# The last two groups' (p x) Wv^T and two more groups' M x in Strassen form, and x1's rows transposed by VectorE and DRAM instead of TensorE

## The chip, the cores and the metric

The kernel runs on one core of a Trainium2 chip. The metric is the device time of the whole program in microseconds, as a median over runs. All data are 32-bit floats. TensorE (PE) does matrix products into PSUM banks of 128 x 512 numbers; VectorE (DVE), ScalarE (ACT) and GpSimd (POOL) do the rest[...]. DMAs are issued from three in-order queues, on SyncE (SP), ACT and POOL, and share 16 DMA engines.

## The reference, cut to what matters

N = 4096 nodes, D = 512 features, H = 128 hidden. Layer 0 is attention with the adjacency matrix added to its scores (twice, as spatial and as edge encoding), then a residual and a layer norm. Layer 1 is a two-layer graph convolution, again with residual and layer norm.

```python
q = x @ Wq.T + bq;  k = x @ Wk.T + bk;  v = x @ Wv.T + bv
a = q @ k.T / sqrt(D) + adj + adj
x1 = layernorm(x + softmax(a) @ v)
h = relu(adj @ (x1 @ W1) + b1)
out = layernorm(x1 + adj @ (h @ W2) + b2)
```

## The kernel before, in words

Queries are taken in 8 groups of 512 (`g`), keys in 8 blocks of 512 (`d`) or 16 pairs of 256 (`q`). Scores are x M x^T with M = Wk^T Wq, so that group g needs `u = M x` (with a bias `ub_t`), 512 x 512. Almost every product is a Strassen-Winograd product: seven half-size products (`ORDER` 1, 2, 6, 7, 5, 4, 3) in place of eight; 1, 6, 5 and 3 go into one PSUM bank (X), 2 and then 7 and 4 into another (Y), and the bank is read out between products. A right-hand operand has seven parts (`B11` ... `T4`), a left-hand one seven others.

*Startup.* Wq and Wk are transposed on TensorE (L848), M is formed (L856, `psm`), and then u of group 0 by plain products (`u_products`, L262, 16 products of 128 x 512). Groups 2 to 7 get their u from `u_fast` (L234, 28 products of 128 x 256, from sums of M in `m_sums`), group 1 from `u_products`, all as filler between the score products of group 0. The parts of u go to DRAM (`store_u`, L176 and L178) and are loaded when their group comes. `sum_x` (L349) forms sums of x for later, in three slots of `t_sb`.

*Groups.* The program is a list of units, each with seven places; a group lasts 16 units. At each place TensorE does one half of a score product (`qk`, L436; VectorE reads it at L449). `hooks` put other work at a given unit and place. `work` is a list of filler items, each with an estimated time, dealt out evenly over the places: the products p x of the previous group (`px_items`, L576, 224 items of 0.43 us, over 128 x 256) and, first among them, the rows of the group before that one's end (`row_items`, L754). Softmax (shift L479, exponential L483, sums L492) and the sums for p x (L519 to L531) are hooks.

*Rows.* For groups 0 to 5 (`FAST_V`) `rows_out_fast` (L659) does (p x) Wv^T in Strassen form: `s3` and three other sums on VectorE, 28 products of 128 x 256 (L703), read by VectorE at L671. Groups 6 and 7 use `rows_out` (L642): 16 products of 128 x 512 (L651). A group has four row tiles (`r`) of 128 rows. Each is normed (`rows_norm`, ACT), gets b2 and goes to DRAM (`add_b2`), is transposed by four TensorE transposes into a bank (`project`, L740) and copied out by ACT (L742, tile `x1t`), and multiplied by W1 into `t_sb` (`project2`, L749). Group 7's rows run inside layer 1: `put(n, ...)` places them beside product n of its first block, with the single bank `m1`.

*Layer 1* is a row of Strassen blocks (L1041) with loads of adj^T and sums on VectorE (L1008 to L1016), then plain products (L1342), the product with W2 and the last norm.

## Time and profile before

| | |
|---|---|
| median of 3 runs | 2306.16 us (2304.3 to 2306.61) |
| the profiled execution, and its span | 2308.84 us, 2307.1 us |
| TensorE products busy | 2276.3 us, 99% of the span |
| VectorE, GpSimd, ScalarE busy | 1617.0, 1018.7, 399.8 us |
| moved by DMA | 525.14 MB, 228 GB/s over the span |
| TensorE clock granted | 0.998 |

A product of two 32-bit operands is two matrix records in the profile, a transpose is one. Records overlap, so the cost of one is the distance between starts, not its own duration. A line such as `PE x1ps L740 <- ACT xr L639: 2.3, 6, 0.4` in the view of waits says: TensorE, at line 740, waited for line 639 on ACT for 2.3 us in total, 6 times, 0.4 us at most. In windows, (x94) is the number of instructions.

### The profile page before, as it was taken

What the parts mean: (1) busy time and instruction counts of PE and PEld (TensorE: products, weight loads), DVE (VectorE), ACT (ScalarE), POOL (GpSimd) and SP (SyncE); (2) the same over time, 40 slices, a digit from 0 to 9 for tenths busy, and PEclk for the clock granted to TensorE, in tenths of its full rate; (3) what the DMA queues carried; (4) which work ended last, traced back from release to release, by engine and by line L of the source; (5) the groups of instructions that cost most, each with busy time, mean ns of one, the idle gap of its engine ahead of it and who ended that gap; (6) DMA issues with size and microseconds to landing.
All of it is one profiled execution on the core that took longest, in us unless ns stands there. A gap on an engine that the chain in (4) does not pass through costs nothing.

```text
span 2307.1 us, 28475 instructions
## 1 busy us (share of the span) xinstructions
PE 2276.3 (99%) x10672; PEld 1750.6 (76%) x10672; DVE 1617.0 (70%) x2276; ACT 399.8 (17%) x438; POOL 1018.7 (44%) x1009
## 2 busy tenths in 40 slices
PE   9999999999999999999999999999999999999998
PEld 5888788888888888888888888888876743333456
DVE  4676776687667756765776687568657877888864
ACT  2212211131122112111311121122102000000012
POOL 3565654185327424731653274237429830001043
PEclk9999999999999999999999999999999999999999
DMA  6999878667857684777578586947754468899996
GB/s 177 273 284 309 233 215 230 193 174 215 246 135 218 189 246 114 215 213 215 151 221 232 145 218 193 259 117 210 196 191 155 155 237 321 332 347 375 352 383 218
DMA packets 282711, 525.14 MB, mean 228 GB/s; under 512 B 23184, under 2 KB 130448, under 8 KB 281680
## 3 DMA queue, kind: packets, MB, share of 16 engines
q1 hardware_dynamic: 229040, 406.12, 52.3%
q0 software_dynamic: 43296, 105.39, 20.7%
q10 hardware_dynamic: 10240, 11.82, 1.7%
q8 instruction: 85, 1.39, 0.2%
q14 instruction: 50, 0.41, 0.0%
HBM read 475.27 MB, written 46.41 MB: 226 GB/s over the span
## 4 chain that ended last, share of the span: by engine, by line
PE 92%; DVE 4%; POOL 2%; DMA 1%; issue 1%; ACT 0%; SPq 0%; POOLq 0%; DVEq 0%; ACTq 0%
PE p L576 32%; PE X L436 18%; PE b L1041 15%; PE Y L436 14%; PE v L703 3%; PE acce L1342 2%; PE psu L234 2%; PE ops L1296 1%; PE tps L749 1%; PE psu L262 1%; PE x L651 1%; PE x1ps L740 1%; DVE s L449 1%; PE psm L856 1%; DMA u_d<-uo 1%
## 5 line engine op out<-in xcount | busy, mean ns | idle before, releaser
L576 PE MATMUL p<-s,xn 128*128 128x256 f32 x3584 | 895.6, 380 | 7.0 <-DVE s L531 2.6
L576 PEld LDWEIGHTS p<-s,xn 128*128 128x128 f32 x3584 | 677.1, 190 | 111.0 <-DVE s L531 5.6
L436 PE MATMUL X<-ut,sa 128*128 128x256 f32 x1984 | 513.4, 381 | 1.7 <-DVE s L449 1.7
L492 POOL TENSOR_TENSOR lacc<-lacc,s 128x512 f32<-128x512 f32 x240 | 344.1, 1434 | 203.2 <-ACT s L483 192.3
L436 PEld LDWEIGHTS X<-ut,sa 128*128 128x128 f32 x1984 | 370.1, 190 | 64.2 <-DVE s L449 15.3
L449 DVE TENSOR_TENSOR s<-X,s 128x512 f32<-128x512 f32 x256 | 176.3, 689 | 278.6 <-PE X L436 278.2
L436 PE MATMUL Y<-ut,sa 128*128 128x256 f32 x1408 | 361.6, 380 | 0.2 <-DVE s L449 0.2
L436 PEld LDWEIGHTS Y<-ut,sa 128*128 128x128 f32 x1408 | 266.8, 190 | 37.7 <-issue 1.4
L483 ACT ACTIVATE s<-s 128x1024 f32<-128x1024 f32 x128 | 135.3, 1057 | 790.3 <-DVE s L479 790.3
L458 DVE TENSOR_TENSOR macc<-macc,s 128x512 f32<-128x512 f32 x240 | 258.1, 1075 | 1.2
L449 DVE TENSOR_TENSOR s<-Y,s 128x512 f32<-128x512 f32 x192 | 131.9, 687 | 157.0 <-PE Y L436 155.7
L479 DVE TENSOR_TENSOR s<-s,mb 128x512 f32<-128x512 f32 x256 | 231.2, 913 | 2.4 <-ACT mb L399 2.4
L385 POOL DMA_DIRECT2D s<-in_adjT_dram x64 | 84.4, 1318 | 256.7 <-ACT s L380 255.9
L549 DVE TENSOR_TENSOR ot<-p,ot 128x512 f32<-128x512 f32 x248 | 168.9, 681 | 31.4 <-PE p L576 31.2
L1008 DVE TENSOR_TENSOR tt<-ck 128x1024 f32<-128x1024 f32 x112 | 138.4, 1270 | 38.7 <-PE b L1041 33.6
L1041 PE MATMUL b<-tt,st 128*64 128x512 f32 (+1 forms) x768 | 156.0, 541 | 0.0
L380 ACT COPY s<-cb 128x2048 f32<-128x2048 f32 x64 | 121.0, 1890 | 48.1 <-PE p L576 39.8
L519 POOL TENSOR_TENSOR s<-s 128x256 f32<-128x256 f32 x128 | 124.6, 974 | 0.6
L1041 PEld LDWEIGHTS b<-tt,st 128*64 128x64 f32 x768 | 53.9, 137 | 87.8 <-issue 79.9
L526 DVE TENSOR_TENSOR s<-s 128x512 f32<-128x512 f32 x128 | 114.3, 914 | 0.0
L520 POOL TENSOR_TENSOR s<-s 128x256 f32<-128x256 f32 x128 | 107.8, 842 | 10.0
L489 POOL TENSOR_TENSOR lacc<-s 128x512 f32<-128x512 f32 x8 | 10.6, 1321 | 197.9 <-ACT s L483 197.9
(186 smaller groups left out, 2112.6 us busy)
## 6 DMA issues: line engine op xcount, KB each, us to landing
ck<-in_adjT_dram SPq DMA_DIRECT2D x128, 1024.0 KB, 7.4
s<-in_adjT_dram POOLq DMA_DIRECT2D x64, 1024.0 KB, 11.5
sa<-s_d SPq DMA_DIRECT2D x224, 256.0 KB, 5.7
xn<-in_x_dram SPq DMA_DIRECT2D x192, 256.0 KB, 4.3
xn<-xs_d SPq DMA_DIRECT2D x96, 512.0 KB, 5.7
sa<-in_xT_dram SPq DMA_DIRECT2D x168, 256.0 KB, 4.7
xn<-xs_d SPq DMA_DIRECT2D x64, 256.0 KB, 3.9
ut<-u_d SPq DMA_DIRECT2D x49, 256.0 KB, 7.2
```

The source lines that it names most:

```text
L380: nc.scalar.copy(s, CB[g].unsqueeze(1).to_broadcast([P, 4, W]))
L436: nc.tensor.matmul(T["X" if k in (1, 6, 5, 3) else "Y"][:, ts(j, HW)], SA[g, d, a][:, c, j, :], UT[g, b][:, c, :], start=k in (1, 2, 7) an ...
L449: nc.vector.tensor_tensor(ck, ps, ck, ALU.add)
L458: nc.vector.tensor_tensor(MACC[g], MACC[g], ck[:, h, :], ALU.max)
L479: nc.vector.tensor_tensor(ck, ck, MB[g], ALU.subtract)
L483: nc.scalar.activation(ck, ck, AF.Exp, scale=2.0)
L492: nc.gpsimd.tensor_tensor(LACC[g], LACC[g], ck[:, h, :], ALU.add)
L519: nc.gpsimd.tensor_tensor(b12, b12, b11, ALU.subtract)
L549: nc.vector.tensor_tensor(to, ps, to, ALU.add)
L576: nc.tensor.matmul(T["PX" if k in (1, 6, 5, 3) else "PY"][:, ts(f, HW)], XN[n][:, q - a, ts(f, P)], quarters(g, q)[{1: 0, 2: 2, 6: 1, 7: 0 ...
L1008: nc.vector.tensor_tensor(t[:, :2], v[:, :, 1], v[:, 0], ALU.subtract)
L1041: nc.tensor.matmul(BK[n][k][ts(half, HH)], lhs, right(u, i, half, b), start=q == 0, stop=q == NP - 1,)
```

## The change

It has four parts.

1. `FAST_V` covers all eight groups. Group 6 uses `rows_out_fast` in its old place; its sums go to GpSimd (`sum_`). Group 7 uses it beside layer 1's first block with `alone`: order 2, 1, 6, 5, 3, 7, 4, all in the bank `m1`, each product read (`j == 2`) two places after it is issued and the next issued two places later.
2. For groups 0 to 5 the transposes leave TensorE. `turn_blocks` lets VectorE transpose the sixteen 32 x 32 blocks of each 128-column part; `store_blocks` writes them to DRAM in four DMAs on SP whose runs are 32 numbers (128 bytes), which puts the blocks in their places; `load_blocks` loads the row tile back. This is moved 70 and more items later in the list.
3. u of groups 0 and 1 also comes from `u_fast`; group 0's directly into its operands. The sums of M, the scores' first sums and the constants of group 0 move into the startup, whose products are reordered. The tile of u is stored in other pieces: B21 by itself from ACT's queue, the rest two products earlier than before.
4. In group 0, `sum_x` is loaded two units ahead instead of one, with five slots instead of three, and `store_s` is issued later.

```diff
-    FAST_V = range(NG - 2)
+    FAST_V = range(NG)
...
+        if what == B21:
+            nc.scalar.dma_start(u_d[b][:, what], UO[b][what])
...
-            nc.gpsimd.dma_start(u_d[b][:, 1:6], UO[b]["all"])
+            nc.gpsimd.dma_start(u_d[b][:, 2:6], UO[b]["all"])
...
+                if b:
+                    store_u(b, B11)
+                    store_u(b, "all")
             if k == 3:
-                store_u(b, "all")
+                if b:
+                    store_u(b, B21)
...
+        sum_ = (nc.gpsimd if g >= NG - 2 else nc.vector).tensor_tensor
...
+        if j == 2:
+            read(k)
+            if k == 1:
+                sum_(a11, a21, a11, ALU.subtract)
+                sum_(a12, a12, a11, ALU.subtract)
+            if k in (3, 4):
+                stats(0 if k == 3 else 2)
+            return
+        if (k, j) == ((2, 0) if alone else (1, 0)):
             read_px()
             T["s3"] = rowp.tile([P, 2, HW], F32, tag="x1t", name=f"s3_{g}")
-            tt(T["s3"], a11, a21, ALU.subtract)
-            tt(a21, a21, a22, ALU.add)
+            sum_(T["s3"], a11, a21, ALU.subtract)
+            sum_(a21, a21, a22, ALU.add)
...
+    def turn_blocks(g, r):
+        T["x1t", g, r] = rowp.tile([P, ND, P], F32, tag="x1t", name=f"x1t{g}_{r}")
+        nc.vector.transpose(T["x1t", g, r].rearrange("p c i -> p (c i)"), XR[g][:, r, :])
+
+    def store_blocks(g, r):
+        x1t = T.pop(("x1t", g, r))
+        to = xt_d[g, r].rearrange("(b i) c (a j) -> a i c b j", i=32, j=32)
+        for a in range(4):
+            nc.sync.dma_start(
+                to[a], x1t[ts(a, 32)].rearrange("i c (b j) -> i c b j", j=32)
+            )
+
+    def load_blocks(g, r):
+        T["x1t", g, r] = XR[g][:, r, :].rearrange("p (c i) -> p c i", i=P)
+        nc.sync.dma_start(T["x1t", g, r], xt_d[g, r])
...
+        if g < NG - 2:
...
+                *w(1), item(0, rows_last, g), *norm(2), *norm(3), *w(8), *norm(0), *w(2), *norm(1), *w(70),
+                *b2(2), *w(3), *turn(2), *w(5), *store(2), *b2(3), *w(11), *turn(3), *load(2), *w(5),
+                *store(3), *b2(0), *w(11), *turn(0), *load(3), *pro2(2), *w(5), *store(0), *b2(1),
+                *w(11), *turn(1), *load(0), *pro2(3), *w(5), *store(1), *w(11), *load(1), *pro2(0),
+                *w(14), *pro2(1),
...
-    first = u_products(0)
...
+    for f in u_fast(0):
...
-    work[0] = 3, [(0.86, f) for f in u_products(1)]
-    work[3] = 13, [(0.86, f) for g in range(2, NG) for f in u_fast(g)] + [(0, lambda: owing.pop()())] * 2
+    work[1] = 15, [(0.86, f) for g in range(1, NG) for f in u_fast(g)] + [(0, lambda: owing.pop()())] * 2
...
-        at(2 * d, 1, store_s, d)
+        at(2 * d + 1, 0, store_s, d)
...
-        at(max(q - 1, 0), 0, sum_x, q)
+        at(max(q - 2, 0), 0, sum_x, q)
...
+    for n, k in enumerate((2, 1, 6, 5, 3, 7, 4)):
+        for j in range(2):
+            put(8 + 4 * n, rows_out_fast, g, k, j, True)
+        put(10 + 4 * n, rows_out_fast, g, k, 2, True)
     for r in range(PER):
-        for c in range(ND):
-            put(9 + 6 * r, rows_out, g, r, c)
...
-        put(35 + 6 * r, project, g, r)
-        put(38 + 6 * r, project2, g, r)
-    put(60, sum_t, 8, 14, 16)
...
+        put(46 + 5 * r, project, g, r)
+        put(49 + 5 * r, project2, g, r)
+    put(66, sum_t, 8, 14, 16)
```

## The prediction

> **What bounds the kernel now.** I read the page first (busy shares, slices, chain), then TensorE's waits, then windows by stage.
>
> ```profile
> PE 2276.3 (99%) x10672; PEld 1750.6 (76%) x10672; DVE 1617.0 (70%) x2276; ACT 399.8 (17%) x438; POOL 1018.7 (44%) x1009
> ...
> PE 92%; DVE 4%; POOL 2%; DMA 1%; issue 1%; ACT 0%; SPq 0%; POOLq 0%; DVEq 0%; ACTq 0%
> ```
>
> TensorE is busy from 3.99 us on, at a granted clock of 0.998, and is 92% of the chain: a product taken away is worth its own time wherever nothing else then ends last. Only 2307.1 - 2276.3 = 30.8 us are idle, and the waits name about half of that (in the view of waits: total, times, longest):
>
> ```profile
> PE X L436 <- DVE s L449: 4.1, 5, 1.0
> ...
> PE x1ps L740 <- ACT xr L639: 2.3, 6, 0.4
> PE psu L234 <- ACT uo L211: 1.9, 1, 1.9
> PE x1ps L740 <- ACT x1t L742: 1.5, 1, 1.5
> ...
> PE x L651 <- DVE xr L656: 0.9, 1, 0.9
> PE tps L749 <- ACT x1t L742: 0.7, 1, 0.7
> ```
>
> The timeline gives the prices (start us, us):
>
> ```profile
> 29.21 10.47 PE L262 MATMUL psu<-xt,m_t 128*128 128x512 f32 x24
> 39.52 1.03 PE L436 MATMUL X<-ut,xt 128*128 128x256 f32 x4
> 40.38 1.02 PE L262 MATMUL psu<-xt,m_t 128*128 128x512 f32 x2
> ...
> 1736.09 0.60 PE L740 MATMUL x1ps<-ident,xr 128*128 128x128 f32 x4
> 1736.53 1.03 PE L576 MATMUL p<-s,xn 128*128 128x256 f32 x4
> ```
>
> Twelve products of 512 columns (two records each) take 39.52 - 29.21 = 10.31, so 0.86 each; two of 256 (four records) 0.86, so 0.43 each; a row tile's four transposes 0.44.
>
> **The change, part by part.**
>
> *Products.* 16 of 0.86 (13.76) become 28 of 0.43 (12.04): -1.72 for each of four groups (u of 0 and 1, rows of 6 and 7), -6.9. *Transposes:* 24 tiles of groups 0 to 5, 24 x 0.44 = -10.6; `project2` stays. Together -17.4 us of TensorE work.
>
> *Waits that go.* The six of 0.4 before L740 (-2.3). The waits 1.5 and 0.7 of group 6, whose norms and transposes get twelve px items between them instead of six, and the 0.9 on the bank of `rows_out` (-3.1). The 1.9 at L234 is ACT waiting for the store of u's tile; that store now goes out two products earlier (-1.9). Of the 4.1 at L436, VectorE waits 9.7 us in group 0 for `t_sb` rows that come late from DMA (L408), and the scores queue behind them; loading these a unit earlier should take half (-2.0, ends 0 and -4.1). Sum -9.3.
>
> *Startup.* Reordered, but TensorE has the same products plus those above. `u_fast` alone accumulates into X every second product; the other bank's product (1.72) covers ACT's read (2 x 0.47) or VectorE's (0.68). The sums of M cost VectorE and GpSimd 0.69 and 1.3 to 1.6 each, beside M's last products. Scores of group 0 start at 37.6 by this, 1.9 earlier; adj's first tile was sent at 32.53, after ACT's copy, and now goes earlier. Cost 0, up to 2 if that tile is late.
>
> *VectorE's transpose* has no row. A copy of 128 x 512 (L822) takes 0.69; the Trainium skill ("VectorE: DVE Perf Modes", the three transpose paths) gives 311 ns for 128 x 128 in 16 bits, by which four parts would be 1.24, an estimate. I take 0.7: 24 x 0.7 = 17 us (30 at the other end) of an engine that is busy 60 to 75% there, so it lies under TensorE's work. ACT loses 24 copies of 0.59, idle anyway.
>
> *The round trip through DRAM* is the dear unknown. Each tile adds four stores and a load to SP's queue: 120 issues more, 0.35 to 0.7 each (four s_d stores take 2.3 to 3.3), ahead of `sa`, `xn` and `ut` loads, which run five operands (19 us) or three phases (21 us) ahead. A store of four DMAs is 2048 runs of 128 bytes, 128 per DMA engine. There is one tile buffer (`x1t`), so `turn(3)` waits on VectorE for `store(2)` to have landed, with all score reads (L449) behind it and TensorE behind those; `load(2)` waits for it on SP. Room: 11 px items and the score halves dealt between them, 11 x 0.43 + 4.7 x 0.86 = 8.8 us. The nearest row is `c_d`, 512 runs of 4 bytes:
>
> ```profile
> c_d<-c_sb ACTq DMA_DIRECT2D x7, 2.0 KB, 9.8
> ```
>
> In the window 329.4 to 340 that holds one, the answer of the DMA view reads
>
> ```profile
> DMA  0001700011100000003130211102123501055420
> ...
> q1 hardware_dynamic: 130, 0.14, 14.4%
> q10 hardware_dynamic: 528, 0.00, 2.4%
> ```
>
> The 528 packets take 0.024 x 16 x 10.6 us = 4.1 us, 8 ns each (17 in the busier window at 130 to 150); yet SP's loads (q1) crawl for some 10 us after. That is the rule that speaks against this change: the Trainium skill ("DMA: Bandwidth & Descriptors", Specifications) says that below 512 bytes the engine reads, modifies and writes. If a 128-byte run costs what a 4-byte run does here, 10 us / 528 = 19 ns each, one after the other, a tile blocks all DMA for 2048 x 19 ns = 39 us; beyond 20 us of lead that starves TensorE for 19 us, 24 times, +450. By the packets' own time, 17 to 30 ns (estimate from the 17 and the 84 of a q1 packet of 1.8 KB: 52.3% of 16 x 2307 us over 229040), it is 128 x 17 to 30 = 2 to 4 us, with issue and receipt some 7, inside the 8.8. I take the latter: c_d writes single words side by side into one 2 KB row, this one whole runs spread over 256 KB. But c_d of the next group goes out beside `store(2)`, so one hold in each group of about 2 us is likely. X and Y alternate, so a read may be some 3 us late free of charge: +3 in all, ends 0 and +450.
>
> *Group 6.* Three sums on GpSimd in a row (1.27 to 1.72 each, L732's rows) stand before product 6, 4.1 with their hand-overs, against 3.44 for products 1 and 2; they stood on VectorE at 0.69. +1.2 (0 to 3); the fourth may stand behind L492 and L519, +0.5.
>
> *Group 7.* One bank: each of seven reads must land within two places (1.7 us); VectorE has idle time at these places (2 to 4 us before each L656). +1 (0 to 5).
>
> *Group 0's stage.* TensorE asks for the same bytes in 3.6 us less:
>
> ```profile
> 60.00:250.00 190.00, 183.13 (x820) 154.74 (x819) 130.29 (x201) 38.97 (x63) 119.44 (x125) 0.99 0.99 294
> ...
> 500.00:750.00 250.00, 249.57 (x1176) 216.99 (x1175) 176.44 (x245) 47.12 (x45) 124.57 (x115) 1.00 0.74 207
> ```
>
> In the first row (columns: length, busy TensorE, weight loads, VectorE, ACT, GpSimd; clock, DMA share, GB/s) DMA is at 0.99, later at 0.74. Giveback +1 (0 to 3.6).
>
> Sum: -17.4 - 9.3 + 3 + 1.7 + 1 + 1 = -20.0. From the profiled span 2307.1 that is 2287.1; the profiled execution's 2308.84 is 2.7 above the median 2306.16, so the median goes to 2286, and I say **2287 us**.
>
> **The rivals.**
>
> *The stores hold VectorE (slower).* One mechanism: a store lands later than 8.8 us after it is sent, `turn` of the next tile holds VectorE, the score reads are late and TensorE stops when they are over 3 us late. Three turns in six groups: 18. At 15 us a store costs 18 x (15 - 11.8) = 58: 2345; it decides from 18 x 1.1 = 20, that is from 12.9 us; by the c_d price it is beyond 2700. For it: c_d's crawl, and VectorE 90% busy (18.02 of 20) at 500 to 520. Against: packet times.
>
> *Half is given back.* Group 0 stays DMA-bound (+3.6, and its 4.1 stay) and the single bank and GpSimd's sums cost their upper ends: 2287 + 2.6 + 2 + 6 = 2298. For it: the 0.99. Against: VectorE's slack in layer 1.
>
> *No change.* The freed TensorE time turns into waits because VectorE, 17 to 30 us heavier, ends last in the px stage: 2304 to 2308. Against: TensorE waits there under 1 us in 250.
>
> **How the numbers follow.** Likeliest 0.60 (its own range 2280 to 2295), half given back 0.16, no change 0.05, slower 0.19. A measurement of this kernel tells about 0.2% (4.6 us) from nothing: faster means below 2301.5. So faster 0.76, same 0.05, slower 0.19. 2279 to 2309 leaves out the slower case and little else.
>
> **What would show it.** Right: 96 fewer transposes into x1ps; TensorE busy about 17 us less; no wait of VectorE's transposes on DMA above 3 us; store landing 5 to 9 us; first score product near 37.6. Wrong: DMA slices near 0 after each store; the score products (L436 before, L412 after) waiting for VectorE in groups 1 to 6; landing of `sa` and `xn` past 15 us; a new wait of seven at group 7's bank.

## The result, and the profile after

The changed kernel takes 2310.81 us (median of 15 runs, 2308.25 to 2314.53) against 2304.55 us before (15 runs, 2304.09 to 2306.61). The ratio is 1.0026, with an interval of 1.0019 to 1.0032: 0.3% slower, where 2287 was forecast. All lines below are those of the changed file: L412 and L425 are the score product and its read, L552 the product p x, L502 and L507 VectorE's sums for it, L525 its read, L434 the maxima, L455 the shift, L468 GpSimd's sums of the exponentials, L740 the turning on VectorE, L758 the product of the turned rows.

TensorE does have less to do. The page of the profile after (busy time and chain, as in the prediction's first view):

```profile
PE 2265.4 (98%) x10672; PEld 1758.8 (76%) x10672; DVE 1621.7 (70%) x2314; ACT 391.5 (17%) x422; POOL 1014.0 (44%) x1007
...
PE 88%; DVE 8%; DMA 2%; issue 1%; POOL 1%; SPq 0%; ACT 0%; POOLq 0%; DVEq 0%
```

It is busy for 10.9 us less than the 2276.3 of before (some 17 were forecast), in a span of the same length (2307.1 in both profiled executions), so its idle time grew from 30.8 to 41.7 us; VectorE's share of the chain doubled from 4% to 8%. The view of waits of the kernel after (who waited at which line for whom: total, times, longest):

```profile
PE p L552 <- DVE ot L525: 9.1, 8, 1.4
DVE x1t L740 <- issue: 7.5, 2, 4.1
PE p L552 <- DVE s L507: 5.7, 10, 0.9
...
PE p L552 <- DVE s L502: 3.3, 8, 0.7
PE X L412 <- DVE macc L434: 2.3, 1, 2.3
...
PE tps L758 <- DMA xr<-xt_d: 1.5, 1, 1.5
```

```profile
DVE x1t L740 <- DMA xt_d<-x1t: 38.2, 10, 6.0
```

The 0.4s before the transposes and the 4.1 at the score product are gone. In their place p x waits for VectorE, and it does so at the same two or three places in each of groups 1 to 6. Before, p x waited for VectorE too, but never in groups 1 to 6 (in that file L526 and L531 are the sums, L549 the read):

```profile
PE p L576 <- DVE s L531: 2.6, 2, 1.7
PE p L576 <- DVE s L526: 2.3, 5, 0.7
...
PE p L576 <- DVE ot L549: 1.4, 2, 0.9
```

VectorE in its turn is held at L740 for 45.7 us, 38.2 of it by the stores of the turned tiles and 7.5 without a named cause. The stores and loads themselves (from the page's DMA issues: count, KB, median us to landing) are quick, with c_d as slow as before:

```profile
xt_d<-x1t SPq DMA_DIRECT2D x96, 64.0 KB, 5.8
xr<-xt_d SPq DMA_DIRECT2D x24, 256.0 KB, 6.3
...
c_d<-c_sb ACTq DMA_DIRECT2D x7, 2.0 KB, 10.1
```

The second window of the prediction, for the kernel after (length; busy TensorE, weight loads, VectorE, ACT, GpSimd; clock, DMA share, GB/s):

```profile
500.00:750.00 250.00, 247.52 (x1157) 215.12 (x1157) 175.65 (x251) 44.77 (x42) 116.61 (x108) 1.00 0.76 205
```

Here, in the midst of groups with rows, TensorE was busy for 249.57 us before and is for 247.52 now: a stage that was full has got holes.

Where the time goes is seen best from the turn of the maxima (TensorE's four transposes of `macc`, once per group, in the timeline). Three profiles, cut there (us):

| profile of | to the first turn | next stretch (no rows yet) | six stretches with rows | from the eighth turn to the end | span |
|---|---|---|---|---|---|
| before | 237.4 | 197.7 | 1280.5 | 591.5 | 2307.1 |
| before, second profile (e_before2) | 235.2 | 197.7 | 1280.4 | 591.6 | 2304.8 |
| after | 228.1 | 201.1 | 1287.3 | 590.6 | 2307.1 |

The front gained 7.1 to 9.3 us and gave 3.4 back at once; the end gained 1.0. The six stretches, where 24 times four transposes were taken from TensorE, became 6.8 us longer.

Part of the first two columns is TensorE's clock. It is granted in full nearly everywhere, but in some places it stands at half for 3.41 us (now and then for twice that), and records then start 0.43 us apart instead of 0.22. Each time costs about 1.7 us. In all profiles TensorE had idled for 1.7 us or more in the 12 us ahead of it; but not every such wait is followed by it (one of 1.9 us in e_undo2 isn't). In the first profile of before one stands right behind the wait of 1.9 us at L234, in the profile of after one stands behind the wait of 2.3 us for the maxima (the window's third figure from the end is the clock):

```profile
143.77 1.13 PE L234 MATMUL psu<-xt,ms_t 128*128 128x256 f32 x4 [1.91 <-ACT uo L211]
144.74 1.80 PE L436 MATMUL Y<-ut,sa 128*128 128x256 f32 x4
146.33 1.91 PE L234 MATMUL psu<-xt,ms_t 128*128 128x256 f32 x4
```

```profile
227.53:230.93 3.40, 3.40 (x12) 2.77 (x11) 0.75 (x2) 0.00 (x0) 1.90 (x3) 0.50 1.03 422
```

The second profile of before has none there; that makes 1.7 of the 2.2 us between its front and the first one's. In the six stretches of these three profiles the clock is full throughout, so the 6.8 us are not of this kind. For the runs below it is said where their six stretches have such places.

### The profile page after: what moved, and what is told of

Same layout as the page of the kernel before. It is cut to its first block, busy times and chain, and to the rows that moved or that the text cites. A ratio compares the mean times of both kernels' runs of the same rounds, so it can differ in the third digit from the quotient of the medians.

```text
span 2307.1 us, 28708 instructions
## 1 busy us (share of the span) xinstructions
PE 2265.4 (98%) x10672; PEld 1758.8 (76%) x10672; DVE 1621.7 (70%) x2314; ACT 391.5 (17%) x422; POOL 1014.0 (44%) x1007
## 4 chain that ended last, share of the span: by engine, by line
PE 88%; DVE 8%; DMA 2%; issue 1%; POOL 1%; SPq 0%; ACT 0%; POOLq 0%; DVEq 0%
PE p L552 28%; PE X L412 18%; PE b L1076 15%; PE Y L412 13%; PE psu L251 4%; PE v L694 4%; PE acce L1379 2%; DVE s L507 2%; DVE s L455 2%; DVE s L502 2%; PE ops L1333 1%; PE tps L758 1%; DVE s L425 1%; DVE ot L525 1%; DVE macc L434 1%
## 5 line engine op out<-in xcount | busy, mean ns | idle before, releaser
L552 PE MATMUL p<-s,xn 128*128 128x256 f32 x3584 | 898.2, 380 | 20.7 <-DVE ot L525 9.1
L552 PEld LDWEIGHTS p<-s,xn 128*128 128x128 f32 x3584 | 676.5, 190 | 128.5 <-DVE ot L525 14.8
L412 PE MATMUL X<-ut,sa 128*128 128x256 f32 x1984 | 514.8, 383 | 3.5 <-DVE macc L434 2.3
L468 POOL TENSOR_TENSOR lacc<-lacc,s 128x512 f32<-128x512 f32 x240 | 345.6, 1440 | 183.1 <-ACT s L459 172.5
L412 PEld LDWEIGHTS X<-ut,sa 128*128 128x128 f32 x1984 | 371.4, 190 | 66.8 <-DVE s L425 16.3
L425 DVE TENSOR_TENSOR s<-X,s 128x512 f32<-128x512 f32 x256 | 176.3, 689 | 264.8 <-PE X L412 259.7
L412 PE MATMUL Y<-ut,sa 128*128 128x256 f32 x1408 | 360.8, 379 | 1.5 <-DVE s L455 1.5
L412 PEld LDWEIGHTS Y<-ut,sa 128*128 128x128 f32 x1408 | 266.8, 190 | 37.5 <-DVE s L455 1.8
L425 DVE TENSOR_TENSOR s<-Y,s 128x512 f32<-128x512 f32 x192 | 131.9, 687 | 174.7 <-PE Y L412 174.0
L434 DVE TENSOR_TENSOR macc<-macc,s 128x512 f32<-128x512 f32 x240 | 232.6, 969 | 1.0
L455 DVE TENSOR_TENSOR s<-s,mb 128x512 f32<-128x512 f32 x256 | 222.7, 877 | 0.7 <-ACT mb L375 0.7
L525 DVE TENSOR_TENSOR ot<-p,ot 128x512 f32<-128x512 f32 x248 | 168.9, 681 | 25.5 <-PE p L552 25.2
L1043 DVE TENSOR_TENSOR tt<-ck 128x1024 f32<-128x1024 f32 x112 | 138.1, 1267 | 35.8 <-PE b L1076 30.8
L502 DVE TENSOR_TENSOR s<-s 128x512 f32<-128x512 f32 x128 | 125.8, 998 | 0.0
L465 POOL TENSOR_TENSOR lacc<-s 128x512 f32<-128x512 f32 x8 | 10.6, 1320 | 200.1 <-ACT s L459 200.1
```

The lines of the kernel that those rows point to most:

```text
L412: nc.tensor.matmul(T["X" if k in (1, 6, 5, 3) else "Y"][:, ts(j, HW)], SA[g, d, a][:, c, j, :], UT[g, b][:, c, :], start=k in (1, 2, 7) an ...
L425: nc.vector.tensor_tensor(ck, ps, ck, ALU.add)
L434: nc.vector.tensor_tensor(MACC[g], MACC[g], ck[:, h, :], ALU.max)
L455: nc.vector.tensor_tensor(ck, ck, MB[g], ALU.subtract)
L468: nc.gpsimd.tensor_tensor(LACC[g], LACC[g], ck[:, h, :], ALU.add)
L502: nc.vector.tensor_tensor(b, b, t2, ALU.subtract)
```

## Experiments: which part costs the time

**One part undone.** In e_undo2 the row lists of groups 0 to 5 are the old ones:

```diff
-        if g < NG - 2:
+        if False:
             turn, store, load = (
```

> The kernel after, but x1's rows of groups 0 to 5 are turned by TensorE again, in the old places; all other parts stay. From here on two theories stand against each other. Theory V (VectorE): what was taken off TensorE stood between the px products 18 to 60 us behind the turn of the maxima, and was the time in which VectorE caught up; with it gone, px waits for VectorE there (0.64, 0.39 and 1.35 us per group), and the way through DRAM costs next to nothing. Theory H (holds): the stores hold VectorE (45.7 us in all) and crowd the DMA queues, and TensorE pays for that. Both say the same of this run: the six stretches from one turn of the maxima to the next, 6.8 us longer in the profile of after than before, come back to 210 to 214.5 us each, the waits on L502, L507 and L525 in groups 1 to 6 go, and the time is 2310.8 - 6.8 = 2304, or as low as 2298 if the 9.3 us of group 0's stage are kept whole (2304.6 - 9.3 + 3.3). If it stays above 2308, part 2 isn't what costs the time, and both fall.

2302.27 us (20 runs, 2301.57 to 2304.94), ratio to before 0.9986 (0.9979 to 0.9993). The six stretches take 1280.1 us, as before; the rest of the change keeps its net gain of 2 to 3 us. The waits of p x in groups 1 to 6 are gone; those that are left stand outside these groups:

```profile
PE p L552 <- DVE s L502: 2.1, 5, 0.7
PE p L552 <- DVE s L507: 1.9, 4, 0.9
```

Turning the rows late without TensorE costs 8.5 us, where it should have gained about 10.

**The holds taken away.** In e_two_bufs every second turned tile goes to another pool:

```diff
-        T["x1t", g, r] = rowp.tile([P, ND, P], F32, tag="x1t", name=f"x1t{g}_{r}")
+        pool, tag = (sap, "sa") if r % 2 else (rowp, "x1t")
+        T["x1t", g, r] = pool.tile([P, ND, P], F32, tag=tag, name=f"x1t{g}_{r}")
```

> The kernel after, but every second turned tile goes to a buffer of the sa pool, so that no turn waits for the store just before it. Theory H: the 45.7 us of holds of VectorE go, and with them what TensorE pays: the waits for VectorE in groups 1 to 6 (2.4 us each, 14 in all) and the pace lost around them; 2291 to 2297. Theory V: the holds cost TensorE nothing, since they stand 100 us behind the turn of the maxima and the waits at 27 to 55: the holds go from the profile, the waits on L507, L502 and L525 stay at 0.64, 0.39 and 1.35 per group, and the time stays at 2309 to 2312.

2310.68 us (14 runs), ratio 1.0021 (1.0013 to 1.0029). The wait of VectorE at L740 for the store is gone from its profile, and TensorE's waits stay:

```profile
PE p L552 <- DVE ot L525: 9.0, 8, 1.4
PE p L552 <- DVE s L507: 5.7, 10, 0.9
PE p L552 <- DVE s L502: 4.0, 10, 0.7
```

So 45.7 us of holds of VectorE cost nothing here. Theory H falls for this kernel.

**The way through DRAM left out.** In e_no_turn the turning, the stores and the loads are gone, all places kept:

```diff
-                lambda r, f=f: [item(0, f, g, r)] for f in (turn_blocks, store_blocks, load_blocks)
+                lambda r, f=f: [item(0, f, g, r)] for f in (no_turn, lambda g, r: None, lambda g, r: None)
```

> The kernel after without VectorE's transposes, without the stores and loads of xt_d, everything else and every place kept; it leaves out the turning of x1's rows of groups 0 to 5, so that layer 1 gets wrong rows. What the new way costs in all, with the dealing of the kernel after. Theory H (stores, loads, holds): 2290 to 2297. Theories P and V: the way itself costs nothing, since what is lost lies 40 to 70 us behind the turn of the maxima, ahead of it: the waits on L507, L502 and L525 stay at 0.64, 0.39 and 1.35 per group, 2307 to 2311.

2307.5 us (21 runs), ratio 1.001 (1.0003 to 1.0016). The way through DRAM with VectorE's transposes costs 2310.8 - 2307.5 = 3.3 us. But against e_undo2 this kernel does strictly less, 10.6 us of TensorE work less, and is 5.2 us *slower*. Its waits are those of the kernel after:

```profile
PE p L552 <- DVE ot L525: 9.2, 8, 1.4
PE p L552 <- DVE s L507: 5.7, 10, 0.9
...
PE p L552 <- DVE s L502: 2.9, 7, 0.7
```

So what ate the gain is neither the turning nor the transfers. It lies in what left the stretch of the px products, and in what was dealt into its place. Not only the transposes left it: in before they and their four products with W1 stand 31 to 52 us behind the turn of the maxima (4 x 0.44 + 4 x 0.86 = 5.2 us per group), and now these products come at 125 to 168 us.

## Experiments: pauses or places

A dealer hands out the items of a list (each entered with an estimated time) evenly over the 112 places of a group, which the expectations call gaps. If items leave the front of the list, all px items behind them come earlier. From the list: px item 28 of a group falls into place 29 in the kernel before and in e_undo2, into place 24 in the kernel after. So two things changed together: TensorE's pauses from px for x1's items are gone, and px is dealt three to five places earlier. The next kernels take these apart.

**VectorE's transpose alone, in the old places** (e_free_turn), and **the pauses put back** (e_dummy):

```diff
         def pro(r):
+            if g < NG - 2:
+                return [item(0, turn_blocks, g, r)]
             return [item(0.44, project, g, r)]
```

> The kernel after, but groups 0 to 5 keep the old order of their rows, and where TensorE's four transposes stood there is VectorE's transpose alone: no store, no load. It leaves out the moving of the 32 x 32 blocks, so layer 1 gets wrong rows. This is what the removed transposes would be worth with the way through DRAM for nothing. Theory H: all of the 10.6 us and the waits for ACT (2.3) are gained over the kernel with TensorE's transposes: about 2298 - 13 = 2285, at most 2292. Theory V: the stretch is VectorE's, which has 2.8 us more to do in each group and 1.76 us less of pauses: the gain of 10.6 turns into waits for VectorE in the same place, and the time is 2298 to 2308, at most 3 us below the run with TensorE's transposes.

2328.2 us (4 runs), ratio 1.0098: 26 us over e_undo2, far outside both expectations. Two things had been changed besides the engine. The 0 in the list moved the px items again, and VectorE now waits at the turning for ACT's normed row (6.4 us) and for releases that the profile doesn't name (17.8 us). Score products wait 14.1 us, up to 2.6 at a time, also without a named cause. Some 8.5 of the 26 us are half clock, five times in the six stretches.

```diff
-... *norm(3), *w(8), *norm(0), *w(2), *norm(1), *w(70),
+... *norm(3), *w(2), *dum(), *w(2), *dum(), *w(4), *norm(0), *w(2), *norm(1), *dum(), *w(4), *dum(), *w(66),
```

> The kernel after, with four times four transposes of the identity (which nobody reads) put back on TensorE in each of groups 0 to 5, two before and two behind the last norms, near where x1's transposes stood: 24 x 0.44 = 10.6 us more of work. Theory V: the pauses come back, the waits for VectorE (2.4 us and some 0.5 of restarts per group) shrink by as much as is put in before them: 0 to +4 us, 2310 to 2315. Theory H: the waits have another cause, and the work adds its full 10.6: 2320 to 2322.

2324.1 us (5 runs), ratio 1.0082: 13.3 more than after, more than the work put in. It doesn't decide: in the profile 8.5 us are half clock, the items also moved px by one or two places, and a new wait of 14.3 us (5 times, up to 3.4) for the loads of turned rows at L758 came up, next to 9.6 at L507. Pauses put in this way are no cure.

**One number of the dealer** (e_deal_only from e_undo2, e_free_dealt from e_free_turn); no instruction is added or removed:

```diff
-            return [item(0.44, project, g, r)]
+            return [item(0 if g < NG - 2 else 0.44, project, g, r)]
```

> The run e_undo2 (TensorE's transposes, 2302.3) with one number changed: the row items of groups 0 to 5 that issue TensorE's four transposes are entered in the dealer's list with 0 us in place of 0.44. No instruction is added or taken away; the dealer gives a gap between two score halves 0.9996 us of items in place of 1.0154, and so deals px items 14 to 84 one to two gaps earlier. Theory P (place): the waits of the px products for VectorE come from where px items fall among the gaps at which shift, maxima and sums are due; then this run pays as e_free_turn did: lost time of 1 to 3.5 us per group, 2308 to 2323. Theory V (VectorE has too much to do where the TensorE items went): nothing changes, 2301 to 2304.

2321.39 us (5 runs), ratio 1.007 (1.0056 to 1.0083): 19.1 us from an estimate of 0.44 entered as 0. The waits: 8.1 us at L502, 4.3 at L507, and 5.6 without a named cause; 3.4 us are half clock.

```diff
-                return [item(0, turn_blocks, g, r)]
+                return [item(0.44, turn_blocks, g, r)]
```

> The run e_free_turn (VectorE's transposes alone in the old places, blocks not moved, so that layer 1 gets wrong rows; 2328.2) with one number changed: VectorE's transpose is entered in the dealer's list with the 0.44 us that TensorE's transposes had, so that every px item falls into the gap into which it fell before. Theory P: the waits on L502 and L507 and the waits of the score products without a named cause go, and the removed 10.6 us of TensorE work show at last: 2302 - 10.6 - 2 = 2290, at most 2296. Theory V: VectorE still has its 17 us more in that stretch, and the run stays above 2315.

2312.33 us (7 runs), ratio 1.0031: the number gives back 15.9 of the 26 us. What is left goes with the turning, where VectorE now waits 38.8 us in all for ACT and unnamed releases; X's products wait 10.2 us for their reads (7 times), px 6.8 us at L502, and 1.7 us are half clock.

**The places of before for the kernel after, and the places of after for e_undo2.** Items that issue nothing keep the count:

```diff
+            pro2 = lambda r: [item(0, project2, g, r)]
...
-... *norm(3), *w(8), *norm(0), *w(2), *norm(1), *w(70),
+... *norm(3), *w(2), *pause(0.44), *w(2), *pause(0.44),
+    *w(1), *norm(0), *w(1), *pause(0.9), *norm(1), *w(2), *pause(0.44), *w(2), *pause(0.9), *w(2),
+    *pause(0.44), *w(2), *pause(0.9), *w(4), *pause(0.9), *w(62),
```

> The kernel after, with items that issue nothing (0.44 and 0.9 us in the dealer's count) where x1's transposes and their products stood before, and its late products entered with 0: the same instructions as after, with every px item in the gap into which it fell before. Theory P: the waits on L507, L502 and L525 in groups 1 to 6 (2.4 us each) go, and what is left of part 2 is its gain: 2302 - 10.6 - 2, plus 1 to 4 for loads that come late: 2290 to 2294, which would be faster than both kernels. Theory V: as after, 2308 to 2312.

2343.9 us (4 runs), ratio 1.0174. Both theories missed by 30 us and more; 10.3 us of that are half clock in the profile. The px waits did shrink (L502 2.4, L507 2.2, L525 1.4 us), but

```profile
PE X L412 <- DVE s L425: 39.3, 25, 5.6
```

the score products now wait for their own reads: at 42 and 68 us behind the turn, where places hold a score half and nothing beside it, and at 124 to 127, behind a hold of VectorE.

> The run e_after_dealt (2343.9) with a second buffer for every other turned tile, as in e_two_bufs. In that run's profile a score product waits 2.7 to 5.6 us for VectorE in each group at 124 to 127 us behind the turn of the maxima, and 0.6 to 0.8 at 155, right behind the holds; where px items are dealt as in the kernel after, the same holds cost nothing. If the holds are the cause there, the waits go and the time is 2343.9 - 6 x 5.2 = 2311 to 2315. If they stay, something else binds the score products there, and the time is above 2335.

2328.39 us (4 runs), ratio 1.0101: the second buffer (the edit of e_two_bufs) takes 15.5 us off, and the longest of these waits falls from 5.6 to 3.2 us, but 34.0 us of them stay. It doesn't take the holds away, though. VectorE stands at the turning for 48.6 us in this profile, against 54.6 in that of e_after_dealt; only the named cause changed, from the stores to none (11 times) and to a load of x (once). Of the 9.0 us between the two profiles 6.8 are half clock. So this run doesn't tell what the holds cost in this order of work; that the waits at 122 to 157 us stand right behind them makes it likely that they cost something here.

```diff
-... *norm(3), *w(8), *norm(0), *w(2), *norm(1), *w(70),
+... *norm(3), *slow(8), *norm(0), *slow(2), *norm(1), *slow(8), *w(62),
```

> The kernel after with two buffers and with the px items dealt as before, but without empty gaps: the first 18 px items behind the rows are each entered with 0.73 us in place of 0.43 (so that every later px item falls into its old gap), and the late products with 0. Same instructions as after. Theory P: the three waits of the kernel after go, as do those at 42, 50 and 68 us of e_after_dealt, which come from gaps that hold a score half alone: 2302 - 10.6 - 2, plus up to 6: 2289 to 2296. Theory V: VectorE misses its pauses however px is dealt: 2308 to 2315.

2329.17 us (4 runs), ratio 1.0102. Theory P in its plain form falls with this: the px items stood in their old places to within one, and TensorE still waited 1.6 to 2.3 us per group for VectorE, or for ACT's copy, between 41 and 69 us (2.1 to 2.4 in the kernel after). The rest of the loss is not the place of px: 5.1 us are half clock, and some 20 us are score products that wait at 122 to 155 us, where VectorE is held at the turning for 48.0 us in all. A place is not a time: where the list counts items that issue nothing, a place is shorter for TensorE, and what VectorE owes at that place is not.

```diff
+            pro = lambda r: [item(0, project, g, r)]
+            pro2 = lambda r: [item(0, project2, g, r)]
+            pause = [item(0.9, lambda: None)]
...
+                *w(4), *b2(1), *w(83), *pause, *w(16), *pause, *w(16), *pause, *w(14), *pause,
```

> The run e_undo2 (TensorE's transposes in the old places among the px items, 2302.3) with the counts of the kernel after: the transposes and their products are entered with 0 us, and items of 0.9 us that issue nothing stand late, where the kernel after has its late products. So the same instructions as e_undo2, with every px item in the gap that it has in the kernel after, three to six gaps earlier (px item 28 in gap 24 instead of 29). Theory P (place): waits of px for VectorE of 2.4 us or more per group between 40 and 75 us behind the turn of the maxima, though TensorE has all of its old work there: 2302 + 6 x 2.4 to 2.9 = 2316 to 2320. Theory V (VectorE misses the time that TensorE's transposes gave it): that time is given here: 2301 to 2304.

2351.72 us (4 runs), ratio 1.0202 (1.0188 to 1.0216): TensorE has all its pauses, and it is 49 us slower than the same instructions dealt as before, with the clock full in all six stretches. Theory V in its plain form falls too. The waits:

```profile
PE p L552 <- DVE ot L525: 16.6, 14, 1.4
PE p L552 <- DVE s L502: 16.4, 16, 1.9
PE X L412 <- DVE s L425: 8.0, 13, 0.8
```

and the windows of that kernel at 65 to 80 us behind a turn of the maxima (columns as above):

```profile
715.09:720.09 5.00, 3.96 (x18) 2.82 (x16) 5.00 (x5) 0.00 (x0) 4.61 (x5) 1.00 1.01 214
720.09:725.09 5.00, 2.58 (x11) 1.97 (x12) 5.00 (x7) 1.06 (x1) 3.21 (x4) 1.00 1.03 264
725.09:730.09 5.00, 3.57 (x17) 2.83 (x16) 5.00 (x6) 0.00 (x0) 4.28 (x4) 1.00 0.57 185
```

VectorE is busy for 5.00 of 5 us in these three windows, where TensorE stops longest (not in all: at 135 to 140 us it is busy for 2.18, and TensorE for 4.22). The same view of the kernel after, at 60 to 70 us, and of before, at 60 to 65 us behind its turn:

```profile
703.67:708.67 5.00, 4.61 (x22) 3.75 (x21) 5.00 (x9) 0.93 (x1) 1.27 (x2) 1.00 1.10 254
708.67:713.67 5.00, 3.65 (x18) 2.89 (x17) 5.00 (x6) 0.13 (x1) 4.64 (x4) 1.00 0.67 231
```

```profile
708.67:713.67 5.00, 5.00 (x25) 4.41 (x24) 5.00 (x6) 1.61 (x2) 4.83 (x5) 1.00 1.03 214
```

In the kernel before VectorE was full as well, with GpSimd at 4.83 (in the next window, at 65 us, 4.88 and 3.42); TensorE just didn't need its reads so early. Note how few instructions fill the second window of after: six in 5.00 us is 0.83 each, against 0.68 for one alone. The timeline of the kernel after shows why (start, duration, engine, line):

```profile
708.85 0.42 DVE L507 TENSOR_TENSOR s<-s 128x256 f32<-128x256 f32 x1
708.87 3.20 POOL L468 TENSOR_TENSOR lacc<-lacc,s 128x512 f32<-128x512 f32 x2 [3.86 <-ACT s L459]
...
709.19 1.76 DVE L455 TENSOR_TENSOR s<-s,mb 128x512 f32<-128x512 f32 x1
...
710.87 1.75 DVE L434 TENSOR_TENSOR macc<-macc,s 128x512 f32<-128x512 f32 x1
...
712.54 0.68 DVE L525 TENSOR_TENSOR ot<-p,ot 128x512 f32<-128x512 f32 x1
...
713.27 0.48 PE L552 MATMUL p<-s,xn 128*128 128x256 f32 x1 [1.35 <-DVE ot L525]
```

L455 and L434 take 1.76 and 1.75 us while GpSimd's two sums run beside them; L525, for which TensorE waits, comes 2 us late for that and takes its usual 0.68. The wait on L507, 43 us behind the turn, is of the same kind, although the window around it isn't full (VectorE 3.3 of 5 us). VectorE is busy without a break up to the L507 that TensorE needs, and two of the instructions ahead of it are long:

```profile
682.48 1.50 DVE L507 TENSOR_TENSOR s<-s 128x256 f32<-128x256 f32 x1
...
683.90 1.75 DVE L455 TENSOR_TENSOR s<-s,mb 128x512 f32<-128x512 f32 x1
...
686.18 0.41 DVE L507 TENSOR_TENSOR s<-s 128x256 f32<-128x256 f32 x1
```

## Experiments: VectorE's time, and what makes it long

**Work taken out of the stretch.** Eight maxima in each of groups 1 to 7, which nobody waits for until the turn, go 36 places later. No px item, row item or count moves:

```diff
-                at(s0 + 2 * d + 2 + n // 7, n % 7, new_max, g, q, h)
+                late = 36 if g and d in (1, 2) else 0
+                at(s0 + 2 * d + 2, n + late, new_max, g, q, h)
```

> The kernel after, in which the maxima over the score tiles of the second and third key block of groups 1 to 7 (8 instructions of VectorE in each group, 0.7 to 2 us each, which nobody waits for until the turn of the maxima) are issued 36 gaps later, out of the stretch 40 to 75 us behind the turn. No px item, no row item and no count of the dealer moves. Theory V', which joins V and P after the runs so far: in that stretch VectorE has more to do than TensorE (5.00 of 5 us in each window with a wait), and the place of the px items only decides how much of it falls together; so with less of VectorE's work there the waits on L507, L502 and L525 go and 2 to 2.9 us per group come back: 2310.8 - 6 x 2 to 2.9 = 2293 to 2299. If they stay as they are (place of the px items alone, or something that isn't VectorE's time): 2309 to 2312.

2301.28 us (21 runs, 2299.08 to 2304.62), ratio to before 0.9983 (0.9977 to 0.999): 9.5 us less than after, short of the 12 to 17 expected. The six stretches fall from 1287.3 to 1278.6. The waits on L525 of groups 1 to 6 are gone, those on L502 fall to 2.1, the one on L507, 43 us behind the turn, stays, and score products now wait 0.4 us per group for their reads at 98 us:

```profile
PE p L552 <- DVE s L507: 5.7, 10, 0.9
PE X L412 <- DVE s L425: 4.5, 10, 0.8
...
PE p L552 <- DVE s L502: 2.1, 4, 0.7
...
PE p L552 <- DVE ot L525: 0.2, 1, 0.2
```

> The same 36 gaps for the same maxima, in the run e_undo2 (TensorE's transposes; 2302.3). There px hardly waits for VectorE in groups 1 to 6. By V' there is little to win: 2300 to 2303; and e_late_max beats it by as much of the 10.6 us of removed transposes as is no longer lost: 2 to 10 us. If the moved maxima themselves harm elsewhere (up to 8 more of them beside the later key blocks), this run shows it: above 2304.

With TensorE's transposes the same edit gives 2300.58 us (14 runs), ratio 0.9982 (0.9974 to 0.999): 1.7 less than e_undo2, within what was expected for it. The second half of the expectation missed: e_late_max doesn't beat it. Even with the maxima gone, turning the rows without TensorE is worth 1280.0 - 1278.6 = 1.4 us in the six stretches of one profile each, and nothing in the medians. So VectorE's time in this stretch explains the waits that went, but moving its eight maxima does not give the 10 us back.

**GpSimd's share of it.**

```diff
-                nc.gpsimd.tensor_tensor(LACC[g], LACC[g], ck[:, h, :], ALU.add)
+                nc.gpsimd.tensor_tensor(LACC[g][:, :P], LACC[g][:, :P], ck[:, h, :P], ALU.add)
```

> The kernel after with GpSimd's running sums of the exponentials taken over 128 of the 512 columns (it leaves out three quarters of the row sums, so the output is wrong). VectorE's instructions are the same and in the same places; only GpSimd, 4.6 to 4.9 us busy of 5 in that stretch, has less to do beside them. If VectorE is slow there because GpSimd works beside it (its maxima take 0.98 us on average and up to 1.75 with GpSimd busy, 0.68 alone), their mean falls below 0.8 and the three waits go: 2293 to 2299. If only the number of VectorE's instructions counts, the mean may fall but the waits stay: 2308 to 2312.

2287.91 us (5 runs), ratio 0.9925 (0.9911 to 0.9938): 22.9 less than after, and below the 2293 to 2299 expected. VectorE has the same instructions in the same order. The two that took 1.76 and 1.75 us, in this kernel's timeline:

```profile
708.31 0.95 DVE L455 TENSOR_TENSOR s<-s,mb 128x512 f32<-128x512 f32 x1
709.18 0.95 DVE L434 TENSOR_TENSOR macc<-macc,s 128x512 f32<-128x512 f32 x1
710.05 0.68 DVE L525 TENSOR_TENSOR ot<-p,ot 128x512 f32<-128x512 f32 x1
```

GpSimd's two sums beside them take 0.71 and 0.79 us in place of 1.52 and 1.60. L434's mean falls from 0.969 to 0.787 us, L455's from 0.877 to 0.742, and in groups 1 to 6 p x no longer waits for VectorE: by the distances between starts a group's px products take 97.5 us, as in before. Part of the 22.9 lies elsewhere: the profiled execution is the slowest of the five, 17.1 less than that of after, with 10.3 in the six stretches and 6.9 in the last one, where GpSimd's shorter sums and px meet too. And TensorE, no longer held up by VectorE, now waits for the turned rows to come back from DRAM:

```profile
PE tps L758 <- DMA xr<-xt_d: 7.0, 5, 2.3
```

So the round trip was cheap in part because TensorE came late. The same cut of GpSimd's sums in e_undo2 wasn't run, so how much of the 22.9 the removed transposes give is open. The view of one line shows which instructions suffer (count; duration in ns, least, median, most), in the kernel after:

```profile
L434 DVE TENSOR_TENSOR macc<-macc,s x240: 651/685/2967, 67.3 to 1714.0; 128x512 f32<-128x512 f32 x120
...
L525 DVE TENSOR_TENSOR ot<-p,ot x248: 672/680/693, 248.4 to 1853.8; 128x512 f32<-128x512 f32 x124
...
L468 POOL TENSOR_TENSOR lacc<-lacc,s x240: 1256/1280/1821, 241.4 to 1832.4; 128x512 f32<-128x512 f32 x120
```

L434 reads two tensors in SBUF and takes up to 2967 ns; L525, of the same size, reads one of its two from PSUM and never takes more than 693. It is so throughout this profile: of the 128 x 512 instructions with one input in PSUM or with a single input (L425, L525, L654, L740) none takes more than 712 ns, while all four lines with two inputs in SBUF (L434, L455, L502 and the half-size L507) have some of about 1.5 us and more. That is what the Trainium skill ("SBUF — State Buffer", the section on SBUF's two separate sides) states: a VectorE instruction with two SBUF inputs and a GpSimd instruction that reads SBUF take a shared port pair as an exclusive lock, and whichever comes second is blocked until the other has finished. The numbers agree: 1.76 - 0.68 = 1.08 us of blocking, less than the L468 of 1.52 us beside it, and 0.95 - 0.68 = 0.27 beside one of 0.71. That the lock is the cause, and not something else that GpSimd does, is the page's word; the runs show only that VectorE's two-input instructions shrink when GpSimd's do.

**What is left of the way through DRAM.** The maxima of e_late_max fall beside the holds at L740. A second buffer for it (the edit of e_two_bufs), or the maxima 60 places later:

> The run e_late_max (2301.3) with a second buffer for every other turned tile. There the maxima now stand 110 to 150 us behind the turn of the maxima, where VectorE is held by the turned tile's buffer (43.0 us in all), and score products wait 0.40 us at 98.5, 0.16 at 117.5 or 0.32 at 152. If the holds cause these, they go, with 0.5 to 1 us per group: 2295 to 2299. If not: 2299 to 2303, and the holds cost nothing in this place either.

2302.44 us (13 runs), ratio 0.9988 (0.998 to 0.9996): no gain. The holds go from the profile; the wait of 0.40 at 98.5 us stays, those at 117 and 152 go. But two waits for loads of turned rows come up (4.6 us), and 1.7 us of half clock, so one can only say that nothing is gained by removing the holds.

> The run e_late_max with the same maxima 60 gaps later in place of 36, behind the holds as well as behind the stretch. If VectorE's time beside the holds is what still costs: 2296 to 2300. If the stretch alone counted: 2299 to 2303. If too many maxima then come shortly before the turn of the maxima, TensorE waits for L434 there (up to 1 to 2 us per group): 2305 to 2312.

2299.86 us (14 runs, 2297.92 to 2302.47), ratio 0.9976 (0.9968 to 0.9984). It is the fastest full kernel of this study, but it is only 0.7 us from e_undo2_late_max, and its distance to both late-maxima runs is within their spreads.

**The second profile of before.**

> The kernel before, unchanged, for a second profile of it: which of its waits in group 0's stage are there in each execution. If the 4.1 us of waits of the score products for VectorE's reads and the 1.9 for ACT at the second bank of u are regular, they show again within 0.3 us; if they hang on when rows happen to arrive, they differ, and the gain of the change in this stage was counted from a bad execution. Theories P and V say nothing of it. Time 2304 to 2306.

2305.23 us (12 runs), ratio 1.0005 (0.9997 to 1.0013). The waits of the score products on VectorE's reads show again (4.2 us, five times), those for ACT at u's bank as 1.6 in place of 1.9. They are regular. The first turn of the maxima came 2.2 us earlier than in the first profile, and 1.7 of that is the half clock that the first one has behind its wait of 1.9 us. So some of the front's gain of 9.3 between the two shown profiles belongs to one execution: it is 7.1 against this one.

## Why the prediction was wrong

*Products, -6.9: about right.* With the transposes on TensorE (e_undo2) it is busy for 2269.6 us, 6.7 less than in the first profile of before and 5.4 less than in the second, which lacks the half clock in the front. *TensorE busy some 17 us less: missed*, it was 10.9 (9.6 against the second profile).

*Startup: right.* The first score product starts at 37.0 to 38.2 us in the profiles with the change, for a forecast of 37.6.

*Waits that go, -9.3: they went, and others came.* The six before the transposes are gone, and the front of the program is 7.1 to 9.3 us shorter (1.7 for each of two u's, 1.9 and 2.0 make 7.3). But the first stretch behind it is 3.4 us longer than before, and 2.3 to 5.9 in the other kernels with the change. In the profile of after 1.4 of the 3.4 are half clock, behind the new wait of 2.3 us for the maxima, and 0.8 are more waits of TensorE, the longest of 1.5 us for VectorE's shift (L455); in e_undo2, with full clock there, the waits are 2.9 us longer. *Giveback +1 (0 to 3.6)* was this term, and it was 3.4, at its upper end; but it was put down to DMA, and the DMA share there (up to 1.08 before, up to 1.09 in e_undo2) doesn't set the kernels apart. In the last stretch, 3.4 us of products and 3.1 of waits less 2.7 made 3.8 forecast; 1.0 came. Its waits only changed their names: 1.3 on L521, 0.8 on L619, 0.7 on the copy of the maxima, for 1.5 on L742, 0.9 and 0.7.

*VectorE's transpose, 0.7: right*, 0.704. *The round trip, +3: right in sum and wrong in its parts.* It costs 3.3 us (e_no_turn). Holds of about 2 us per group were forecast; they are 7.6 per group, with waits of up to 6.0 us for a store where none above 3 was to be seen, and they cost nothing in this kernel (e_two_bufs). The rival "the stores hold VectorE" needed a landing from 12.9 us on. The view of the tensor, which has its stores and loads together, shows that the longest took just this; it is one DMA of a store:

```profile
DMA to landing us min/median/max: 3.0/5.8/12.9
```

*Transposes, -10.6: this is the step that failed.* "A product taken away is worth its own time wherever nothing else then ends last", says the prediction, and then takes it that VectorE, "busy 60 to 75% there", lies under TensorE's work. It also gave no cost to the new order, in which px comes three to five places earlier because x1's items come later. TensorE's x1 items stood 31 to 52 us behind the turn, where VectorE was not yet full (2.4 to 4.3 of 5 us in windows of before). But the px products that took their place need VectorE's sums and reads up to 70 us behind the turn, and there VectorE works without a break, on instructions made long beside GpSimd. So VectorE does end last. By the distances between starts the transposes' 1.9 us per group went, and the px products of a group took 100.3 us in place of 97.4: 2.3 of waits (0.64, 0.39 and 1.35 are the usual ones), the rest lost around them. Net, part 2 was worth +8.5 in place of -10.6 - 2.3 + 3 = -9.9, which is 18.4 off. Taken as a change, the forecast was -20 and the medians say +6.3, some 26 off; the other 7 or 8 are in the other parts, which gained 2 to 3 us (e_undo2) where 10 was forecast: 2.4 of the giveback, 2.8 of the end, and some 2 to which no term could be put.

*The rivals.* "No change: VectorE ends last in the px stage" was the right mechanism, with 0.05, and its 2304 to 2308 was near; but it put this down to the added turning (17 to 30 us), and e_no_turn, without any turning, has the same waits. The argument against it, that TensorE waited there for under 1 us in 250, took the absence of waits for the presence of room: a window of 5 us of the very profile read 5.00 for VectorE and 4.83 for GpSimd. The prediction's windows were 20 to 250 us long, and an average over one of those hides it. The prediction named the mean share of VectorE, but not that some two fifths of its instructions there (L434, L455, L502, L507: 94 of 213 in a group) have two SBUF inputs and grow beside GpSimd.

*What stays open.* It is shown that p x waits for VectorE, and that these waits shrink when VectorE has less to do in that stretch or is less slowed there. Whether they came from the pauses that went or from the earlier places of px isn't shown: no run changed one of the two alone without other waits coming up. Why e_undo2_after_deal and e_after_dealt lose as much as 49 and 33 us was followed only to VectorE's full windows and late reads (and 10.3 us of half clock in the latter). And of the 10.6 us, 1.4 at most shows even with the maxima out of the way; what binds then wasn't tried, beyond the wait on L507 at 43 us and the 0.4 at 98 us.

## What to carry to other kernels

Before taking work off the bounding engine, look at windows of a few us (here 5, not 20 or 250) where that work stands and just behind it: if another engine reads full there, what comes earlier may wait for it, and the removal may be worth nothing. Here moving eight of that engine's instructions out gave 9.5 us back, and still no more than the kernel that kept the transposes. An estimate in a list that deals work out is part of the kernel: one item's 0.44 entered as 0 cost 19 us with not one instruction changed (3.4 of it by the clock), so an edit of such a list should keep the counts, or be tried with the counts changed alone. Where GpSimd works beside VectorE, count VectorE's instructions with two SBUF inputs at their duration in that window, not at the one they have alone.

## What was not expected of the hardware

A VectorE instruction of 128 x 512 with both inputs in SBUF took from 0.65 to 2.97 us in one profile, long where GpSimd's instructions ran beside it, and is counted as busy all that time; so VectorE's busy share rises with GpSimd's work (VectorE 1621.7 us busy in the kernel after, 1507.3 in e_short_sums, with the same 2314 instructions). Where TensorE had just waited 1.7 us or more, its clock was at times halved for 3.41 us, which doubled the distance between its records from 0.22 to 0.43 us. And 96 stores of 64 KB in runs of 128 bytes, 51168 packets under 512 bytes more than before, left other loads nearly as they were: the median landing of the loads of `sa` is 5.7 us with them and 5.2 without (e_no_turn), and the kernels differ by 3.3 us.
